# When layer 1's first edge columns are multiplied inside layer 0's last block: two sixteenths later, and nine of them behind the last expert

## The chip, the cores and the metric

The kernel runs on one NeuronCore of a Trainium2 chip. The metric is device time in microseconds (us) of one execution. The kernel before took 2913.34 us, the median of three runs from 2908.56 to 2917.24. The profile is one further execution, which took 2906.32 us, with a span of 2904.5 us from its first to its last instruction.

The engines have short names in the views: PE is TensorE (PEld its weight loads), DVE is VectorE, ACT is ScalarE, POOL is GpSimd, SP is SyncE, whose queue here only starts DMAs.

## What is computed

Two layers of a graph network with a mixture of experts behind each, on 6,250 nodes of 256 features and 100,000 edges (`src`, `dst`, `edge_weight`, sorted by `dst`). Cut to what matters:

```python
x = x + gnn0(norm(x))                       # gather h at dst, weigh, sum at src
x = x + sum_e gate[e] * mlp_e(norm(x))      # layer 0: 8 experts, all of them for every node
h1 = norm(x)
x = x + segment_sum(edge_weight * h1[src], dst) @ W + bias     # layer 1's aggregation
x = x + expert_top1(norm(x))                # layer 1: 32 small experts, the best one for each node
```

The output is x. Layer 1's aggregation needs rows of `h1` from all over the graph, while layer 0 produces them in order of nodes. This is the seam in which the change lies.

## The kernel before

**Tiles.** The nodes lie in 49 tiles of 128 in the SBUF tensor `X`, which is updated in place. Layer 0 works through them in 15 blocks of 1 to 4 tiles (`blocks0`); the last block, `late`, has three. Layer 1 has 13 blocks of its own (`blocks1`), the first of them three tiles as well.

**Edge columns.** The edges of layer 1, sorted by destination, are cut into 782 columns of 128 edges. One column is five pieces of work, issued by `columns1`:

1. `gather` (L199, its DMA at L201): GpSimd starts an indirect DMA that fetches 128 rows of `h1` from HBM into a tile `g`.
2. `weighted`, first half (L230): ScalarE multiplies `g` by the edge weight into `m[:, 0]`, rounded to fp32r.
3. `weighted`, second half (L231): VectorE computes the rest that the rounding lost into `m[:, 1]`.
4. `one_hots` (L218, L222): VectorE writes, for three columns at a time, the 0/1 matrix `s` that says which edge goes to which node.
5. The product `acc<-m,s` (L277) on TensorE, summed in PSUM over groups of eight columns.

A group that is done is moved by L250 (ScalarE) and added by L251, L255 and L258 (VectorE) into the destination tile's sums. `columns1` hands out these later steps 2, 6 and 9 columns behind the group's end. The pool for the early columns has 12 tiles `g` and 6 tiles `m` (`(3, 12, 6, 2)`: one-hots, gathers, weighted, sums), so gather number k needs the weighting of column k-12 to be over, and weighting k the product of column k-6.

**The early columns.** The first 64 columns (`NE = EARLY * GC`) belong to the first tiles of layer 1. They are multiplied already in layer 0's last block, in `first_sums`, with only those source rows that earlier blocks have written to `h1` (`early_columns` sets the weight of the others to nought). What they miss, edges that come from the last block's own nodes, is added behind that block: `missing` builds matrices for it in three steps beside experts 5 to 7 (iota L822 on GpSimd, `to_m` and `of_m` L858 to L862 on VectorE, `pm` L866 and L867 on TensorE, L868 and L869 on ScalarE), and `add_missing` multiplies them with the last block's rows (`corr` L878) and adds them to `first_sums` (L880). Tiles 0, 1 and 2 of `first_sums` go through `by_weight` (L209 to L215) before layer 1's first block can begin; parts 3 and 4 are wanted only later. A tile takes its columns from half a group before it to half a group behind it: tiles 0 to 2 are complete with the first 52 of the 64 columns.

**The order of the work.** An aggregation is a generator that hands out one column for each `next`; `Stream.upto(n)` (L367) advances it until n columns are out. `aggregate0` (L692) first hands out layer 0's own 882 columns, then the 64 early ones. The loop over experts calls `sums.upto(...)` twice for each of the 8 experts of a block, before the second hidden layer (`hidden0`, L748 and L751) and before the outputs (`outs0`, L760 and L762). These 16 places, the sixteenths of the block, take their targets from `plans[b]`. For the last block they are

```python
head = 2
plans[-1] = [cum[-1] + NE * max(0, u + 1 - head) / (2 * NX0 - 1 - head) for u in range(2 * NX0 - 1)]
plans[-1] += [cum[-1] + NE + 1]
```

so nothing in sixteenths 0 and 1, then 4.9 columns in each, and by the last sixteenth all 64 with their later steps.

The program's text is not yet the order on the engines: a scheduler in the framework takes the instructions with their priorities and their dependences and writes one fixed order for each engine, which then runs in that order, with waits on semaphores. So the plan says from where on columns may be expected, and the scheduler interleaves them.

**At the block's two ends.** The gathers of the early columns need all earlier rows of `h1`. The last of these come from `end0` of the block before (stats, the square root L333 on ScalarE, the normalized rows `hs` L771 on VectorE, the DMA L773 on SP), which runs beside the last block's first expert. At the far end `end0(late)` does the same for the last block; then follow `add_missing`, `by_weight` and `begin1`, layer 1's first block. Layer 1's own gathers read all of `h1`, so the first of them waits for that last L773. SP also carries four loads of layer 1's expert weights into the space of layer 0's: `load1`, L799 (first matrix) and L803 (second), half of each at expert 4 and half at expert 7, each as soon as the old weights have been used for the last time.

Of the kernel before, what the change touches and what calls it, by code (L numbers as in the profile page):

```python
# [24 lines left out]
CS = 8  # L25
# [8 lines left out]
NX0 = 8  # L34
# [15 lines left out]
def gnn_ffn_kernel(ctx: ExitStack, tc: tile.TileContext, a, out):  # L50
# [323 lines left out]
    def aheads(cum, parts, rests):  # L374


        cum = cum + [cum[-1]] * 2
        out, at = [], cum[0]
        for b, rest in enumerate(rests):
            head = parts - rest  # L380
            plan = [at + (cum[b + 1] - at) * (u + 1) / head for u in range(head)]
            plan += [cum[b + 1] + (cum[b + 2] - cum[b + 1]) * (u + 1) / parts for u in range(rest)]
            at = plan[-1]
            out.append(plan)
        return out
# [247 lines left out]
    NE = EARLY * GC  # L633

    with tc.tile_pool(name="layer0", bufs=1) as wp, tc.tile_pool(name="outs0", bufs=1, side="right") as wo_pool, \
# [56 lines left out]
        def aggregate0():  # L692
            for b, tiles in enumerate(blocks0):
                idx, dl, w = edges[b]
                for i, t in enumerate(tiles):
                    acc = psum.tile([P, 2, D], F32, tag="agg", name="acc", bufs=2)
                    for j in range(EW):
                        if j % SJ == 0:
                            s = one_hots(wp, dl[:, i, :], j, 3)
                        m = weighted(wp, h0, idx[:, i, j:j + 1], w[:, i, j:j + 1], 12, 6)  # L700
                        nc.tensor.matmul(acc, s[:, j % SJ, :], m, start=(j == 0), stop=(j == EW - 1))  # L701
                        if j == EW - 1:
                            for half in range(2):
                                nc.vector.tensor_add(X[:, t, :], X[:, t, :], acc[:, half, :])
                        yield

            for _ in columns1(wp, psum, range(NE), h1[:LIM, :], idx_e, w_e, (3, 12, 6, 2)):
                yield
            while True:
                yield  # L710
# [161 lines left out]
        def add_missing(hs, fs):  # L872

            corr = psum.tile([P, 2, D], F32, tag="mm", name="corr", bufs=3)
            for u, f in enumerate(fs):
                rows = min(P, NEAR - f * P)
                for i in range(n_late):
                    nc.tensor.matmul(corr[:rows, u, :], mats[i][:, f * P:f * P + rows], hs[:, i, :],  # L878
                                     start=(i == 0), stop=(i == n_late - 1))
                nc.vector.tensor_add(first_sums[:rows, f, :], first_sums[:rows, f, :], corr[:rows, u, :])  # L880


        sums = Stream(aggregate0())
        cum = [EW * (tiles[-1] + 1) for tiles in blocks0]
        plans = aheads(cum, 2 * NX0, [4] * nblk)
        head = 2
        plans[-1] = [cum[-1] + NE * max(0, u + 1 - head) / (2 * NX0 - 1 - head) for u in range(2 * NX0 - 1)]
        plans[-1] += [cum[-1] + NE + 1]
        sums.upto(cum[0])
        block = begin0(blocks0[0])  # L890
        first = hidden0(0, block, 0, block[1])
# [40 lines left out]
            next(firsts[-1])  # L932
        for part in firsts:
            next(part)
        add_missing(hs, (3, 4))
    sorted_ctx.close()


    with tc.tile_pool(name="layer1", bufs=1, reuse_waits="tile") as wp, \
# [74 lines left out]
        with tc.tile_pool(name="flow1", bufs=1, reuse_waits="tile") as flow:  # L1014

            sums = Stream(columns1(flow, psum, range(NE, NREAL), h1, src_c, val_c, (5, EW + 6, 12, 4)))
            cum = [0] + [min(CS * (2 * tiles[-1] + 2) + CS // 2, NREAL) + LAG - NE for tiles in blocks1[1:]]
            plans = aheads(cum, 2 * NC1, [4] + [8] * (len(blocks1) - 1))
# [90 lines left out]
```

## Time and profile before

| what | us |
|---|---|
| median of three runs | 2913.34 |
| profiled execution | 2906.32 |
| its span | 2904.5 |
| TensorE busy | 2685.0 (92%) |
| VectorE busy | 2017.1 (69%) |
| GpSimd busy | 1921.2 (66%) |
| ScalarE busy | 1626.5 (56%) |
| mean of one L201 gather, layer 0 and early / layer 1 | 1.02 / 1.01 |
| median from a gather's issue to its landing | 2.8 |

How to read the views: a row of a timeline gives the start in us, the busy time in us, engine, line, operation, tiles written and read, the number of instructions in a row, and in brackets the idle time before and what ended it. A row of waits gives who waited for whom, the total in us, how often, and the longest. A row of windows gives, for a stretch from one time to another, each engine's busy time with its instruction count, the granted clock of TensorE as a share of full speed, the share of the DMA engines and GB/s. In the 40 slices a digit is tenths of the slice, in the PEclk row tenths of full clock. An fp32 product shows as two records ("x8" is four products), one in fp32r as one.

The last block of layer 0 runs from about 1722 to 1835 us of the span; layer 1's first gather is issued at 1840.95 us.

### The profile page before, as it was taken

What the parts mean: (1) busy time and instruction counts of PE and PEld (TensorE: products, weight loads), DVE (VectorE), ACT (ScalarE), POOL (GpSimd) and SP (SyncE); (2) the same over time, 40 slices, a digit from 0 to 9 for tenths busy, and PEclk for the clock granted to TensorE, in tenths of its full rate; (3) what the DMA queues carried; (4) which work ended last, traced back from release to release, by engine and by line L of the source; (5) the groups of instructions that cost most, each with busy time, mean ns of one, the idle gap of its engine ahead of it and who ended that gap; (6) DMA issues with size and microseconds to landing.
All of it is one profiled execution on the core that took longest, in us unless ns stands there. A gap on an engine that the chain in (4) does not pass through costs nothing.

```text
span 2904.5 us, 36970 instructions
## 1 busy us (share of the span) xinstructions
PE 2685.0 (92%) x10276; PEld 1750.0 (60%) x10336; DVE 2017.1 (69%) x4917; ACT 1626.5 (56%) x3790; POOL 1921.2 (66%) x1932
## 2 busy tenths in 40 slices
PE   5888848889999999999999998779999999999998
PEld 2444427666566666666666665556666666666666
DVE  8999978788767767667666646566666666666630
ACT  6777837655555555555555545355555555555532
POOL 4666667777767666776675527577777777777720
PEclk9999969999999999999999998989999999999999
DMA  4000043333333333333332214333333333333310
GB/s 150 19 19 19 19 144 97 104 101 101 93 99 96 89 102 93 91 103 95 90 100 82 82 40 126 95 108 100 108 109 109 106 108 102 108 107 109 109 46 12
DMA packets 123140, 260.73 MB, mean 90 GB/s; under 512 B 32236, under 2 KB 68904, under 8 KB 122920
## 3 DMA queue, kind: packets, MB, share of 16 engines
q0 software_dynamic: 79872, 218.21, 26.5%
q1 hardware_dynamic: 31672, 32.42, 3.4%
q10 hardware_dynamic: 11376, 7.60, 0.8%
q8 instruction: 85, 1.39, 0.2%
q14 instruction: 135, 1.11, 0.1%
HBM read 238.87 MB, written 19.25 MB: 89 GB/s over the span
## 4 chain that ended last, share of the span: by engine, by line
PE 60%; DMA 10%; issue 6%; DVE 5%; ACT 3%; POOL 2%; another core or an unknown queue 0%; ACTq 0%; POOLq 0%; SPq 0%; DVEq 0%
PE ph L748 19%; PE py L760 10%; PE py L999 8%; PE ph L983 8%; PE acc L701 6%; DMA g<-h,src_c 5%; PE acc L277 4%; DMA g<-h,idx 3%; POOL g L201 2%; DVE m L231 2%; ACT m L230 2%; DMA g<-h,idx_e 1%; PE ph L214 1%; PE tr L340 1%; PE pl L720 1%
## 5 line engine op out<-in xcount | busy, mean ns | idle before, releaser
L201 POOL DMA_INDIRECT g<-h,idx x882 | 900.0, 1020 | 390.7 <-DVE m L231 171.5
L201 POOL DMA_INDIRECT g<-h,src_c x718 | 724.9, 1010 | 244.2 <-issue 110.8
L230 ACT ACTIVATE m<-g,w 128x256 fp32r<-128x256 f32 x882 | 393.9, 500 | 254.5 <-PE acc L701 130.7
L230 ACT ACTIVATE m<-g,val_c 128x256 fp32r<-128x256 f32 x718 | 349.8, 503 | 278.5 <-PE acc L277 133.2
L751 ACT ACTIVATE hT<-ph,shift,scale 128x512 f32<-128x512 f32 (+3 forms) x480 | 328.8, 696 | 313.4 <-PE ph L748 312.0
L231 DVE SCALAR_TENSOR_TENSOR m<-g,val_c,m 128x256 fp32r<-128x256 f32 x718 | 336.8, 482 | 213.0 <-ACT m L230 209.2
L231 DVE SCALAR_TENSOR_TENSOR m<-g,w,m 128x256 fp32r<-128x256 f32 x882 | 397.3, 476 | 44.4 <-ACT m L230 43.5
L748 PE MATMUL ph<-nT,w 128*128 128x512 f32 (+3 forms) x960 | 376.1, 527 | 25.0 <-ACT hT L751 24.9
L760 PE MATMUL py<-wo,hT 128*128 128x256 f32 x1568 | 379.7, 385 | 14.0 <-DVE X L762 11.4
L999 PE MATMUL py<-w,hm 128*128 128x256 f32 x1568 | 385.2, 384 | 2.0 <-ACT hm L988 1.9
L983 PE MATMUL ph<-nT,w 128*128 128x512 f32 (+2 forms) x832 | 377.2, 574 | 0.0
L701 PE MATMUL acc<-m,s 128*128 128x512 f32 x882 | 339.7, 488 | 37.1 <-DVE scale L657 24.7
L748 PE MATMUL ph<-hT,w 128*128 128x512 f32 (+3 forms) x960 | 369.9, 519 | 0.5 <-ACT hT L751 0.5
L760 PEld LDWEIGHTS py<-wo,hT 128*128 128x128 f32 x1568 | 293.2, 192 | 80.6 <-DVE X L762 28.0
L277 PE MATMUL acc<-m,s 128*128 128x512 f32 x782 | 335.4, 502 | 5.7 <-DVE m L231 5.4
L999 PEld LDWEIGHTS py<-w,hm 128*128 128x128 f32 x1568 | 290.9, 192 | 51.8 <-ACT hm L988 3.9
L222 DVE TENSOR_TENSOR s<-col,dl 128x384 fp32r<-128x384 f32 x294 | 161.3, 550 | 185.7 <-PE acc L701 183.5
L748 PEld LDWEIGHTS ph<-nT,w 128*128 128x128 f32 x960 | 176.9, 197 | 175.1 <-issue 119.6
L748 PEld LDWEIGHTS ph<-hT,w 128*128 128x128 f32 x960 | 175.7, 193 | 118.5 <-issue 89.1
L988 ACT ACTIVATE hm<-ph,b 128x512 f32<-128x512 f32 (+2 forms) x208 | 136.8, 659 | 194.7 <-PE ph L986 141.9
L701 PEld LDWEIGHTS acc<-m,s 128*128 128x128 f32 x882 | 169.2, 195 | 108.9 <-issue 50.1
L983 PEld LDWEIGHTS ph<-nT,w 128*128 128x128 f32 x832 | 158.0, 192 | 102.2 <-issue 81.8
(248 smaller groups left out, 3343.7 us busy)
## 6 DMA issues: line engine op xcount, KB each, us to landing
g<-h,idx POOLq DMA_INDIRECT x882, 2.8
g<-h,src_c POOLq DMA_INDIRECT x718, 2.8
h<-hs SPq DMA_DIRECT2D x25, 256.0 KB, 2.1
X<-in_x_dram SPq DMA_DIRECT2D x12, 512.0 KB, 9.4
out_dram<-o SPq DMA_DIRECT2D x11, 512.0 KB, 3.4
h<-hs SPq DMA_DIRECT2D x9, 512.0 KB, 3.1
w<-in_L_ffn_W_dram ACTq DMA_DIRECT2D x2, 2048.0 KB, 11.9
wo<-in_L_ffn_Wo_dram ACTq DMA_DIRECT2D x1, 2048.0 KB, 21.1
```

The source lines that it names most:

```text
L201: nc.gpsimd.indirect_dma_start(out=g, out_offset=None, in_=h, in_offset=bass.IndirectOffsetOnAxis(ap=idx, axis=0))
L222: nc.vector.tensor_tensor(s[:, :n], col[:, None, :].to_broadcast([P, n, P]), dl[:, j:j + n, None].to_broadcast([P, n, P]), OP.is_equal)
L230: nc.scalar.activation(m[:, 0, :], g, AF.Copy, scale=w)
L231: nc.vector.scalar_tensor_tensor(m[:, 1, :], g, w, m[:, 0, :], op0=OP.mult, op1=OP.subtract)
L277: nc.tensor.matmul(acc, s[:, (j - js.start) % SJ, :], m, start=opens, stop=done)
L701: nc.tensor.matmul(acc, s[:, j % SJ, :], m, start=(j == 0), stop=(j == EW - 1))
L748: nc.tensor.matmul(ph[:, :nw], (w1, w2)[layer][:, e, k, m * P:(m + 1) * P], src[:, k, :nw], start=(k == 0), stop=(k == 1))
L751: nc.scalar.activation(hT[:, m, :nw], ph[:, :nw], AF.Relu, bias=shift[:, layer, c:c + 1], scale=scale[:, layer, c:c + 1])
L760: nc.tensor.matmul(py, hT[:, k, j * P:(j + 1) * P], wo[:, e, k, :], start=(k == 0), stop=(k == 1))
L983: nc.tensor.matmul(ph[:, :nw], w1f[:, k, c * P:(c + 1) * P], nT[:, k, :nw], start=(k == 0), stop=False)
L988: nc.scalar.activation(hm[:, :nw], ph[:, :nw], AF.Relu, bias=b1[:, c:c + 1])
L999: nc.tensor.matmul(py[:, j, :], now[:, cols], w2f[:, c, :], start=False, stop=(c == NC1 - 1), skip_group_check=True)
```

## The change

The plan of the last block gets other numbers, and a line is added behind `by_weight`:

```diff
         plans = aheads(cum, 2 * NX0, [4] * nblk)
-        head = 2
-        plans[-1] = [cum[-1] + NE * max(0, u + 1 - head) / (2 * NX0 - 1 - head) for u in range(2 * NX0 - 1)]
-        plans[-1] += [cum[-1] + NE + 1]
+
+        head, tail = 4, 2 * CS
+        plans[-1] = [cum[-1] + (NE - tail + CS // 2 + 3) * max(0, u + 1 - head) / (2 * NX0 - head) for u in range(2 * NX0)]
@@ behind the last block: end0(late), add_missing for parts 0 to 2, by_weight for tiles 0 to 2
         for part in firsts:
             next(part)
+        sums.upto(cum[-1] + NE + 1)
         add_missing(hs, (3, 4))
     sorted_ctx.close()
```

With `NE` 64, `CS` 8 and `NX0` 8, the targets are: none in sixteenths 0 to 3, then 55 / 12 = 4.6 columns in each of the other twelve, so 55 by the block's end. The other nine columns, with the later steps of the last two groups, are asked for behind `by_weight`, ahead of the corrections for parts 3 and 4. The 55 take in the 52 columns of tiles 0 to 2 and the three by which their last group's sums follow.

## The prediction

> **What bounds the kernel now.** First the page's 40 slices (72.6 us each), to see where TensorE is not full.
>
> ```profile
> PE   5888848889999999999999998779999999999998
> ...
> PEclk9999969999999999999999998989999999999999
> ```
>
> Outside the sort at the start TensorE is nine tenths busy, but for three slices from the 25th on (1743 to 1960 us), where the clock dips too. That is layer 0's last block and the first two of layer 1. Next, the waits of TensorE from the last block's first hidden product (1722.3) to the first correction product (1837.05), and the busy table of the same 114.7 us.
>
> ```profile
> PE py L760 <- DVE X L762: 6.0, 2, 5.6
> PE acc L277 <- DVE m L231: 5.4, 8, 1.0
> PE ph L748 <- ACT hT L751: 4.1, 2, 2.3
> PE pm L866 <- DVE to_m L858: 3.0, 1, 3.0
> PE corr L878 <- DVE hs L771: 2.4, 1, 2.4
> PE pm L866 <- ACT wo L869: 0.7, 1, 0.7
> ```
>
> ```profile
> core 0: us, PE busy (x) PEld busy (x) DVE busy (x) ACT busy (x) POOL busy (x), PEclk, DMA share, GB/s
> 1722.30:1837.00 114.70, 92.54 (x305) 60.12 (x304) 65.54 (x164) 54.63 (x112) 66.63 (x65) 0.91 0.38 114
> ```
>
> The block's work at full clock: a burst of 4 hidden or 6 output products takes 2.58 (starts 1722.33, 1724.91, 1727.49 in the timeline); there are 8 second-layer, 7 first-layer and 8 output bursts, 59.3. 64 column products at 0.33 (1734.48 to 1734.81) are 21.1; 12 pairs of L866 and L867 at 0.35 are 4.2. Sum 84.6, and 84.6 / 0.91 = 93.0 is the busy time shown. So 114.7 is 84.6 of work, 8 of low clock and 22 of waits. Behind whom? VectorE's waits in the same stretch lead with 25.9 us for `m` on ScalarE, and ScalarE's with 35.1 us for the gathers. So GpSimd's timeline, and then the two ends on ScalarE:
>
> ```profile
> 1730.62 0.94 POOL L201 DMA_INDIRECT g<-h,idx_e  x1 [48.90 <-DVE X L762]
> 1731.87 0.95 POOL L201 DMA_INDIRECT g<-h,idx_e  x1 [0.30 <-issue]
> ...
> 1815.39 0.95 POOL L201 DMA_INDIRECT g<-h,idx_e  x1 [0.30 <-issue]
> 1840.95 0.94 POOL L201 DMA_INDIRECT g<-h,src_c  x1 [24.62 <-PE corr L878]
> ```
>
> ```profile
> 1765.31 1.84 ACT L230 ACTIVATE m<-g,w_e 128x256 fp32r<-128x256 f32 x4 [4.24 <-DMA g<-h,idx_e]
> ...
> 1820.94 0.51 ACT L230 ACTIVATE m<-g,w_e 128x256 fp32r<-128x256 f32 x1 [3.49 <-DMA g<-h,idx_e]
> ...
> 1836.13 0.20 ACT L333 ACTIVATE rstd<-rstd 128x3 f32<-128x3 f32 x1 [3.90 <-DVE rstd L332]
> ```
>
> The 64 gathers start at 1730.62 (block 11's rows of h1 must be in HBM: hs at 1727.3 and a DMA of 2.52), run without a gap beyond 0.30, and the last is issued at 1815.39: 84.8 / 63 = 1.35 us each. A column can become a product 3.9 us after its gather starts (1730.62 to 1734.48). The plan of before asks for products from the third sixteenth on, when not one is ready, and then for 5 a sixteenth: TensorE meets the gathers head-on. The two long landings (ScalarE rows 1 and 2) sit at the loads of L799, issued at 1758.37 and 1815.02; the chain shows gathers of 6.31 and 5.47 there, against 2.74 elsewhere. The L803 load at 1773.50 left none over 3.0.
>
> **The change, part by part.** Nothing is added or removed: 64 columns keep their 64 gathers, weightings, one-hots and products, and the queues of SP and GpSimd keep their order but for the iota of L822, which stands behind gather 43 instead of 53. From the norm of layer 1's first block on, the order of all four engines' instructions in the two built programs is the same. So all of it lies between 1733 and about 1850, and what the last block ends earlier, layer 1 starts earlier.
>
> *Products from the fifth sixteenth.* Four sixteenths now run as bare bursts: 1722.33 + 6 x 2.58 = 1737.8, and the fourth column is due at 1734.5 + 3 x 1.25 = 1738.2. The 5.4 us of L277 waits become 0.5. They don't all come back, since later groups of 4 to 5 columns (9.2 per expert, 12.3 us of gathers against 3 x 2.58 + 9.2 x 0.33 = 10.8 of TensorE) again catch up with the gathers. Also ScalarE's order now puts all four relu evictions of an expert behind a run of five or six weightings (the first run ends with column 10, landed about 1745), so the second first-layer burst waits for its PSUM tile there, some 3 us, then 1 to 2 per expert. I charge these to the gather's pace, not twice.
>
> *Nine columns behind the last expert.* In the built program the scheduler pulls five of the nine up again, so 60 products precede the corrections and 4 (1.3 us) follow the first three `by_weight`. TensorE's floor to product 60 is 59.3 + 60 x 0.33 + 4.2 = 83.3, or 1805.6. Its walk with the waits: the first `pm` needs the iota, behind gather 43 at 1730.6 + 43 x 1.33 = 1788, so it runs at 1789; from there 14 outputs (6.0), 12 hidden products (7.7), `pm` (4.2) and 24 columns (7.9), with 1.5 of waits on `to_m`, give 1816.3, and 1815.3 for the last output.
>
> *What sets the end instead.* In ScalarE's order the square root L333 of the last norm now stands behind the weightings of all 64 columns and one eviction (before, weighting 64 was 15 us earlier). A rule of the Trainium skill speaks against the change here: TensorE: Matmul & The Clock Gate, section "Architectural detail", says that ScalarE's and VectorE's queues are strict FIFO. The row agrees in kind: the `m` at 1820.94 held the evictions behind it for 3.49. Without the rule, VectorE's own chain decides: 1.4 from the last output to the root, as before (1834.7 to 1836.1), and four weightings (columns 58 to 61) that now stand between, spaced 0.40: 1815.3 + 1.4 + 1.6 = 1818.3, -17.8. With it: gather 64 issued at 1815.4 as now (nothing upstream of it changes), landed 2.74 later (the second L799 load moves from 1815 to about 1798, off the last gather), weighting 0.51, eviction 0.36, a hand-over of 0.2, so L333 at 1815.4 + 2.7 + 0.5 + 0.4 + 0.2 = **1819.2** against 1836.13: **-16.9**. I take the rule's value.
>
> *Costs.* One VectorE add (L251, 0.42) now stands between reciprocal and hs. Behind hs, L255, two `m` and one `s` (0.41 + 0.96 + 0.55) fall into the 1.74 us in which VectorE waited for corr. Another L251 (0.42) stands ahead of layer 1's reciprocal. The four late products go before corrections that no one waits for. Together +0.8. SP: h1's last rows are written right after hs in both; layer 1's first gather came 3.3 after that issue (1837.66 to 1840.95) and moves along.
>
> *The clock.* The same page, Part 1, says that TensorE falls to half rate after about 3.4 us of idling and needs as long to recover. Here: after the waits around 1751 a burst of 8 records took 4.17 instead of 2.74, 1.4 lost; the rule gives up to 1.7 per lull. The 5.63 lull at 1761 is of that kind, and the change has one such (column 10). By either it is 1.4 to 1.7 on TensorE, early, where the gathers bound; so 0 on the sum, and 2 if it falls after 1789.
>
> Sum: -16.9 + 0.8 = -16.1. The profiled execution took 2906.32 (span 2904.5 and 1.8 around it); the median is 7.0 above it. Against its own time the sum gives 2890.2; off the median, **2897**. Runs spread over 8.7 us, so about 0.3% is what can be told from no change.
>
> **Rivals.**
>
> *A, gathers pace the end* (above): 2897; own range 2892 to 2902. For it: 0.30 gaps throughout, 35.1 us of ScalarE waits.
>
> *B, gathers get faster.* With VectorE and DMA less crowded they keep the early 1.25 (1730.62 to 1731.87): gather 64 at 1730.6 + 78.8 = 1809.4, L333 at 1813.2, -22: 2891. Against it: layer 1's mean is 1.01 + 0.30 too.
>
> *C, half comes back.* Evictions behind weightings, one more lull after 1789 and the L799 load hitting columns 50 to 53 make TensorE the last, by 9 us (three recoveries of 1.4 and an L799 wait of 5): L333 at 1828, 2906.
>
> *D, slower: the ring of buffers.* Gather k needs weighting k-12, and that product k-18. Where TensorE falls over 18 columns behind, gathers stop, and it then waits for them. Break-even is L333 at 1835.3, that is the last gather landing 16 later than 1818.1, or 1.6 us per gather instead of 1.35; at 1.75 the result is 2922. Against it: gather 19 needs product 1, done at 1738 and wanted at 1755; gather 64 needs product 46, done by 1807 in the walk and wanted at 1815.
>
> *E, the wait only moves.* Layer 1's gathers start from other releases and begin1 takes the gain back: 2913. Against it: the order there is the same and its first gather is released by hs's write.
>
> **How the numbers follow.** A 0.58, B 0.13, C 0.19, D 0.06, E 0.04. Faster by over 0.3% (under 2904.6): nearly all of A (0.56), B, and 0.08 of C, 0.77. Slower (over 2922): most of D, 0.05. The rest 0.18. The range 2889 to 2910 holds A, most of B (0.10) and C (0.16).
>
> **What would show it.** Right: first `acc` L277 of the last block at about 1738, L277 waits under 2 us in its first ten columns; last early gather at 1813 to 1817; L333 at 1817 to 1822 with ScalarE's `m` waiting for a gather just ahead; first layer-1 gather near 1824.5. Wrong: a gap over 0.30 between early gathers (D), TensorE waits on `hT` over 12 us or the last outputs well after the last gather's landing (C), or a layer-1 first gather at 1824 with an unchanged end (E).

## The result, and the profile after

The changed kernel takes 2898.59 us (median of eight runs, 2893.99 to 2904.92) against 2912.36 us for the kernel before in the same series (eight runs, 2906.32 to 2917.24). The ratio is 0.9955, with a 95% interval of 0.9943 to 0.9967, so about 13 us less (9.6 to 16.6). Forecast were 2897.0 us and -16.1. A later series gave 2895.83 against 2909.19, ratio 0.9953 (0.9935 to 0.9972). The profiled execution took 2895.13 us, its span is 2893.4.

First the 40 slices of the page of the changed kernel.

```profile
PE   5888848888999999999999998779999999999998
...
PEclk9999978999999999999999999999999999999999
```

The dip behind the 24th slice is still there in TensorE's busy share (8779), but the clock row no longer dips with it. In the fine view this is, from the last block's first hidden product to the first correction product (1726.50 to 1824.14), first TensorE's waits and then the row of windows:

```profile
PE py L760 <- DVE X L762: 4.4, 2, 2.5
PE ph L748 <- ACT hT L751: 3.9, 2, 2.1
PE acc L277 <- DVE m L231: 1.7, 4, 0.8
PE pm L866 <- DVE to_m L858: 1.6, 2, 1.0
```

```profile
1726.50:1824.14 97.64, 84.23 (x301) 56.91 (x301) 61.61 (x159) 52.91 (x111) 66.04 (x65) 0.97 0.43 134
```

The same stretch was 114.70 long with a busy TensorE of 92.54 at a clock of 0.91. TensorE's work in front of the corrections is smaller by only four products (1.3 us). All else in the 17 us is less waiting (13.4 us not busy instead of 22.2, so 8.8) and, as the rest, about 7 us of less low clock.

The stretch starts 4.2 us later in this profile than in the one before (first early gather at 1734.85 instead of 1730.62), after 1.7 ms of unchanged instructions. So times are counted from here on from the first early gather. Now GpSimd's timeline of the changed kernel, the end of ScalarE's, and two rows of TensorE's:

```profile
1734.85 0.94 POOL L201 DMA_INDIRECT g<-h,idx_e  x1 [48.89 <-DVE X L762]
...
1819.01 0.95 POOL L201 DMA_INDIRECT g<-h,idx_e  x1 [0.30 <-DVE X L762]
1828.05 0.95 POOL L201 DMA_INDIRECT g<-h,src_c  x1 [8.09 <-PE corr L878]
```

```profile
1819.80 0.51 ACT L230 ACTIVATE m<-g,w_e 128x256 fp32r<-128x256 f32 x1 [1.63 <-DMA g<-h,idx_e]
1821.58 1.31 ACT L230 ACTIVATE m<-g,w_e 128x256 fp32r<-128x256 f32 x3 [1.28 <-DMA g<-h,idx_e]
1822.79 0.36 ACT L250 ACTIVATE first_sums<-acc 128x256 f32<-128x256 f32 x1
1823.06 0.19 ACT L333 ACTIVATE rstd<-rstd 128x3 f32<-128x3 f32 x1
```

```profile
1818.87 1.13 PE L760 MATMUL py<-wo,hT 128*128 128x256 f32 x4
...
1824.14 1.13 PE L878 MATMUL corr<-hs,wo 128*128 128x256 f32 x4 [1.70 <-DVE hs L771]
```

The gathers run as they did (84.16 us from first to last, before 84.77, every gap 0.30). But the root L333 now follows the last weighting by 0.17 us. The last output of expert 7 (ended 1819.99) no longer decides.

In the kernel before, the last gather's column sat in the middle of the last expert's work. This is VectorE's timeline there, and then two rows of TensorE's:

```profile
1821.49 0.48 DVE L231 SCALAR_TENSOR_TENSOR m<-g,w_e,m 128x256 fp32r<-128x256 f32 x1 [3.12 <-ACT m L230]
1821.89 0.87 DVE L762 SCALAR_TENSOR_TENSOR X<-py,gate,X 128x256 f32<-128x256 f32 x2
1822.67 0.51 DVE L858 TENSOR_SCALAR to_m<-wo,dst_m 128x576 fp32r<-128x576 f32 x1
```

```profile
1823.24 0.50 PE L866 MATMUL pm<-to_m,of_m 128*128 128x512 f32 x1 [3.01 <-DVE to_m L858]
...
1831.35 3.33 PE L760 MATMUL py<-wo,hT 128*128 128x256 f32 x12
```

Read it as a chain: the last gather lands, ScalarE weighs it (the `m` at 1820.94 of the prediction's view), VectorE's `m` follows at 1821.49, behind it in VectorE's queue the `X` adds and then `to_m`, and on that waits TensorE's `pm` at 1823.24. Only then come the rest of the missing rows' products, four columns, expert 7's second layer, its outputs and the statistics. From the end of the last weighting to L333 it is 14.7 us.

The marks of all profiles, in us from the start of the first early gather. "Weighting 64" is the end of ScalarE's last `m`, "last output" the end of expert 7's last product, "sel" the first product of layer 1 with `sel` (L987 in the changed kernel, L986 in the kernel before):

| kernel | last gather issued | weighting 64 | last output | L333 | sel |
|---|---|---|---|---|---|
| before | 84.77 | 90.83 | 104.06 | 105.51 | 129.29 |
| changed | 84.16 | 88.04 | 85.15 | 88.21 | 112.37 |
| changed, again (e5) | 84.17 | 88.08 | 85.15 | 88.25 | 112.36 |
| head alone (e11) | 87.32 | 92.58 | 105.82 | 107.27 | 131.37 |
| *chips with late gathers:* | | | | | |
| head alone (e1 / e6) | 97.3 / 98.1 | 104.9 / 105.6 | 117.2 / 117.8 | 118.6 / 119.3 | 144.2 / 144.8 |
| tail alone (e2 / e7 / e12) | 97.2 / 99.5 / 98.3 | 113.8 / 112.3 / 110.9 | 113.0 / 111.5 / 110.1 | 115.4 / 114.0 / 112.6 | 141.9 / 140.0 / 138.7 |
| tail held behind (e3 / e8) | 97.4 / 101.6 | 116.4 / 120.2 | 105.3 / 109.1 | 106.8 / 110.5 | 134.0 / 137.1 |
| half the gathers (e4 / e9 / e10) | 60.5 / 60.1 / 59.0 | 85.4 / 84.9 / 83.8 | 83.9 / 83.5 / 82.4 | 86.7 / 86.3 / 85.1 | 113.4 / 110.6 / 111.1 |

Ten of the twelve experiments ran on four other chips, on which the kernel before takes 3228 to 3296 us and gathers are issued with gaps of up to 7 us (the last section has more on them). They are compared only among themselves.

### The profile page after: what moved, and what is told of

Same layout as the page of the kernel before. It is cut to its first block, busy times and chain, and to the rows that moved or that the text cites. A ratio compares the mean times of both kernels' runs of the same rounds, so it can differ in the third digit from the quotient of the medians.

```text
span 2893.4 us, 37030 instructions
## 1 busy us (share of the span) xinstructions
PE 2677.7 (93%) x10336; PEld 1750.2 (60%) x10336; DVE 2012.4 (70%) x4917; ACT 1626.1 (56%) x3790; POOL 1926.1 (67%) x1932
## 4 chain that ended last, share of the span: by engine, by line
PE 65%; DVE 17%; DMA 8%; issue 4%; ACT 4%; POOL 1%; ACTq 0%; POOLq 0%; DVEq 0%
PE ph L748 19%; PE py L760 10%; PE py L1000 9%; PE ph L984 9%; PE acc L701 6%; PE acc L277 4%; DMA g<-h,src_c 4%; DMA g<-h,idx 3%; DVE loads L527 3%; DVE to L523 2%; DVE m L231 2%; ACT m L230 2%; PE ph L987 1%; PE ph L214 1%; POOL g L201 1%
## 5 line engine op out<-in xcount | busy, mean ns | idle before, releaser
L748 PE MATMUL ph<-nT,w 128*128 128x512 f32 (+3 forms) x960 | 373.1, 524 | 25.0 <-ACT hT L751 24.8
L760 PE MATMUL py<-wo,hT 128*128 128x256 f32 x1568 | 382.1, 387 | 13.8 <-DVE X L762 10.5
L984 PE MATMUL ph<-nT,w 128*128 128x512 f32 (+2 forms) x832 | 374.8, 571 | 0.0
L748 PE MATMUL ph<-hT,w 128*128 128x512 f32 (+3 forms) x960 | 368.5, 518 | 0.5 <-ACT hT L751 0.5
L277 PE MATMUL acc<-m,s 128*128 128x512 f32 x782 | 332.2, 499 | 1.7 <-DVE m L231 1.7
L748 PEld LDWEIGHTS ph<-nT,w 128*128 128x128 f32 x960 | 175.2, 195 | 174.2 <-issue 118.1
L748 PEld LDWEIGHTS ph<-hT,w 128*128 128x128 f32 x960 | 176.2, 193 | 118.9 <-issue 88.3
L984 PEld LDWEIGHTS ph<-nT,w 128*128 128x128 f32 x832 | 157.2, 191 | 101.5 <-issue 81.1
## 6 DMA issues: line engine op xcount, KB each, us to landing
w<-in_L_ffn_W_dram ACTq DMA_DIRECT2D x2, 2048.0 KB, 11.2
```

Of the source, the lines that this page charges most:

```text
L277: nc.tensor.matmul(acc, s[:, (j - js.start) % SJ, :], m, start=opens, stop=done)
L748: nc.tensor.matmul(ph[:, :nw], (w1, w2)[layer][:, e, k, m * P:(m + 1) * P], src[:, k, :nw], start=(k == 0), stop=(k == 1))
L760: nc.tensor.matmul(py, hT[:, k, j * P:(j + 1) * P], wo[:, e, k, :], start=(k == 0), stop=(k == 1))
L984: nc.tensor.matmul(ph[:, :nw], w1f[:, k, c * P:(c + 1) * P], nT[:, k, :nw], start=(k == 0), stop=False)
```

## The experiments

**The changed kernel again (e5)**, with no edit.

> The changed kernel itself once more. If the chip is one with the times of the case (kernel before near 2912 us), L333 is again 88 us after the first early gather, within 1 us, and the ratio is 0.995 to 0.997. If it is the chip of the experiments so far (kernel before 3284 us, its gathers issued with gaps of up to 6 us where the other had 0.30), theory A says that the end follows the gathers' slower pace in both kernels: L333 100 to 107 us after the first early gather, where head alone had 118.6 and tail alone 115.4, and a gain over the kernel before of 8 to 15 us, 0.995 to 0.998; a rival in which TensorE's own work and waits set the end says 115 or more and no measurable gain.

Measured: 2895.83 against 2909.19, 0.9953 (0.9935 to 0.9972). The marks repeat within 0.05 us. So on such a chip a difference of half a microsecond in them means something, though the whole time spreads over 6 to 17 us from run to run.

**The head alone (e11, e1, e6)**: products from the fifth sixteenth, all 64 columns ahead of expert 7's output as before.

```diff
-        head, tail = 4, 2 * CS
-        plans[-1] = [cum[-1] + (NE - tail + CS // 2 + 3) * max(0, u + 1 - head) / (2 * NX0 - head) for u in range(2 * NX0)]
+        head = 4
+        plans[-1] = [cum[-1] + NE * max(0, u + 1 - head) / (2 * NX0 - 1 - head) for u in range(2 * NX0 - 1)]
+        plans[-1] += [cum[-1] + NE + 1]
...
-        sums.upto(cum[-1] + NE + 1)
```

> The products come from the fifth sixteenth, but all 64 columns stay ahead of the last expert's output and nothing is left behind by_weight. Measured from the start of the first early gather to the end norm's root (L333): 105.5 us in the kernel before, 88.2 in the changed one. Theory A (the 64 gathers pace the end: a head that comes later costs and gains TensorE nothing that the gathers don't give back): the last column's product can be fed about 87 us after the first gather, and the last 12 products of expert 7 and the statistics (some 6 us) follow it: L333 at 93 to 95, so about -11 us, time near 2901. Rival (the head saves only its 5.4 us of waits for m, the rest is the tail's): L333 at 100, time near 2907. Rival C (the head's waits only move elsewhere): L333 at 104 or more, time 2911 to 2914.

> The head part alone, again, where the kernel before takes some 2910 us (on the chip of the first four runs gathers waited for buffers, and both theories' numbers were off). From the first early gather to L333: before 105.5 us, changed kernel 88.2, twice within 0.05. Theory A (gathers pace the end, then expert 7's last outputs): 93 to 95, time 2899 to 2901. Rival (the head saves its 5.4 us of waits for m): 100, time near 2906. Rival C (the waits only move): 104 or more, time 2908 to 2912.

> The head part alone, for a chip on which gathers are issued 0.30 us apart. From the first early gather to L333: kernel before 105.5 us, changed kernel 88.2. Theory A (gathers pace the end, then expert 7's last outputs): 93 to 95, time near 2900. Rival (the head saves its waits for m, 5.4 us, and the tail the rest): 100, time near 2906. Rival C (the waits only move): 104 or more, time 2908 to 2912. If the gathers are late here as on three chips of four so far, L333 is at 118 to 120 again and the time is within 0.3% of the kernel before.

Measured on a chip of the case's kind (e11): 2914.03 against 2909.47, ratio 1.0013 (1.0000 to 1.0026), L333 at 107.27, which is 1.76 later than before. None of the gain is there. Of the three numbers offered for L333, that of rival C holds ("the waits only move"; its time of 2908 to 2912 is passed by 2 us), but for another reason than C's. Its TensorE waits, its row of windows and the end of its ScalarE timeline:

```profile
PE ph L748 <- ACT hT L751: 6.7, 3, 3.0
PE acc L277 <- DVE m L231: 6.0, 2, 4.0
PE py L760 <- DVE X L762: 5.4, 3, 2.6
PE pm L866 <- DVE to_m L858: 3.2, 2, 2.5
PE corr L878 <- DVE hs L771: 2.4, 1, 2.4
```

```profile
1725.68:1842.17 116.49, 92.72 (x306) 61.95 (x304) 65.88 (x164) 54.37 (x112) 69.28 (x65) 0.90 0.38 112
```

```profile
1824.51 0.51 ACT L230 ACTIVATE m<-g,w_e 128x256 fp32r<-128x256 f32 x1 [3.78 <-DMA g<-h,idx_e]
1825.65 0.91 ACT L230 ACTIVATE m<-g,w_e 128x256 fp32r<-128x256 f32 x2 [0.62 <-DMA g<-h,idx_e]
...
1841.25 0.20 ACT L333 ACTIVATE rstd<-rstd 128x3 f32<-128x3 f32 x1 [3.90 <-DVE rstd L332]
```

The waits for `m` did not fall from 5.4 to 0.5; they are 6.0. With the same 64 columns in two sixteenths less, the plan asks for 5.8 of them a sixteenth instead of 4.9 and runs into the gathers a little later and harder. And from the end of weighting 64 (92.58) to L333 (107.27) it is 14.69 us, in the kernel before 14.68 (90.83 to 105.51). As long as all 64 columns stay ahead of expert 7's output, the end hangs on the last gather by the same chain, with either head. The 1.76 us by which it is later are the 1.75 by which weighting 64 is. They come from gathers issued later (2.55 at the last one): two of them took 4.06 and 2.92 us of GpSimd's time, where the longest in the changed kernel is 1.73. The 93 to 95 that I had for theory A had put 6 us of work behind the last column instead of 14.7.

On the chips with late gathers (e1, e6) the ratios are 0.9992 (0.9964 to 1.0019) and 0.9993 (0.9961 to 1.0026), no difference either. L333 lies 13.7 and 13.6 us behind weighting 64.

**The tail alone (e2, e7, e12)**: the last nine columns behind the last expert, products from the third sixteenth as before.

```diff
-        head, tail = 4, 2 * CS
+        head, tail = 2, 2 * CS
```

> The products start two sixteenths earlier, as in the kernel before, and the last nine columns lie behind the last expert. Theory A (the gathers pace the end): TensorE pays its waits for m in the first bursts but catches up while the last gathers land; L333 at 88 to 90 us after the first early gather (changed kernel 88.2), time within 2 us of the changed kernel, near 2899. Rival C (TensorE's own work and waits set the end): the 5.4 us of waits for m and 1 to 3 us for hT come back, L333 at 93 to 96, time near 2905.

> The tail part alone, again. Theory A (the gathers pace the end): L333 at 88 to 90 us after the first early gather, time within 2 us of the changed kernel, near 2897. Rival C (TensorE's own work and waits set the end): 5.4 us of waits for m and some for hT come back, L333 at 93 to 96, time near 2902.

> The tail part alone, for a chip on which gathers are issued 0.30 us apart; the head alone had L333 at 107.3 us after the first early gather there (kernel before 105.5, changed kernel 88.2), ratio 1.0013: nothing of the gain. Theory A (the tail carries it; the gathers pace the end whatever the head): L333 at 88 to 90 us, time within 2 us of the changed kernel, near 2897. Rival C (the head is worth something only with the tail: products that come two sixteenths earlier make TensorE wait for m, 5.4 us, and the waits are not made up before expert 7's outputs): L333 at 93 to 96, time near 2902. If the gathers are late here, L333 is at 114 to 115 again.

All three ran on chips with late gathers: 0.9986 (0.9964 to 1.0009), 0.9971 (0.9951 to 0.9990) and 1.0012 (0.9988 to 1.0036). That is one gain of 0.1 to 0.5% and two that can't be told from nothing. In the marks one thing is as in the changed kernel: the last output comes 0.8 us ahead of the end of weighting 64 instead of 12.2 behind it (e1, e6), and L333 is 3.1 and 5.3 us earlier than with the head alone on the same chips (e2 against e1, e7 against e6). But the gathers do not set the end there. Weighting 64 ends 12.6 to 16.6 us after the issue of the last gather (7.5 and 7.6 with the head alone), and in all three runs the last weightings wait for products to free a tile `m` (for e2 the row at 2014.01 further down). So at the end it is TensorE that the weightings wait for, which is nearer to rival C than to theory A. How much of TensorE's delay goes back to earlier late gathers is not shown. GpSimd's timeline of e2 shows why the numbers expected for the other chip don't apply:

```profile
1965.09 0.95 POOL L201 DMA_INDIRECT g<-h,idx_e  x1 [0.30 <-issue]
1970.68 0.94 POOL L201 DMA_INDIRECT g<-h,idx_e  x1 [4.64 <-DVE m L231]
```

The ring of twelve gather buffers is full, and GpSimd waits for a weighting to free one. From first to last the gathers take 97.2 to 99.5 us, 1.54 to 1.58 each: near the 1.6 that the prediction named as the break-even of its rival D. What the tail alone does where gathers are not late is left open, and with it whether the later head adds anything once the tail has moved.

**The tail held behind the norm (e3, e8)**: the changed kernel, in which the nine tail columns stand behind L333 in ScalarE's order and behind the last hs in VectorE's.

```diff
-        hs = end0(late)
+        hs, behind = end0(late), list(held)
...
-        sums.upto(cum[-1] + NE + 1)
+        with tc.issue_after(behind[0].ins), tc.issue_after(behind[1].ins):
+            sums.upto(cum[-1] + NE + 1)
```

(`held` keeps the instructions of L333 and L771.)

> The changed kernel, with the nine tail columns' weightings held behind the end norm's root on ScalarE and behind its hs on VectorE, so that L333 waits for no gather after column 54. Theory A (in-order queues: L333 stands behind the weightings of all 64 columns): L333 comes 2 to 6 us earlier, at 82 to 86 us after the first early gather, the corrections and layer 1's first gather with it, time 2894 to 2897. Rival C (TensorE's last outputs set L333, the weightings ahead of it are hidden): L333 at 87 to 88 and the nine columns then come later than before, so that by_weight and begin1 wait: time 2898 to 2904.

> The nine tail columns' weightings held behind the end norm's root on ScalarE and behind its hs on VectorE, again. Theory A (L333 stands behind 64 weightings): L333 at 85 to 86.5 us after the first early gather instead of 88.2 (expert 7's last output ended at 85.15 in the changed kernel with two products ahead of it), the corrections 2 us earlier; and the first layer-1 gather 2 us earlier, at 91. What the nine columns then cost behind the corrections was 3 us on the other chip (24.2 us from L333 to layer 1's first sel product became 27.3): time between the changed kernel's and 2 us more. Rival C (TensorE's last outputs set L333): L333 at 87.5 or later, time 2 to 4 us above the changed kernel.

The numbers of both theories miss, since gathers were late. What can be read is the order of queues. ScalarE's timeline at the end of e2 (tail alone) with the row of L332, on which L333 waits, and ScalarE's of e3:

```profile
2014.01 0.51 ACT L230 ACTIVATE m<-g,w_e 128x256 fp32r<-128x256 f32 x1 [0.62 <-PE acc L277]
2015.51 0.38 ACT L250 ACTIVATE first_sums<-acc 128x256 f32<-128x256 f32 x1 [0.99 <-PE acc L277]
2016.20 0.20 ACT L333 ACTIVATE rstd<-rstd 128x3 f32<-128x3 f32 x1 [0.32 <-DVE rstd L332]
```

```profile
2015.63 0.46 DVE L231 SCALAR_TENSOR_TENSOR m<-g,w_e,m 128x256 fp32r<-128x256 f32 x1
2016.00 0.17 DVE L332 TENSOR_SCALAR rstd<-mv 128x3 f32<-128x3 f32 x1
```

```profile
1994.40 0.20 ACT L333 ACTIVATE rstd<-rstd 128x3 f32<-128x3 f32 x1 [4.22 <-DVE rstd L332]
1994.51 2.49 ACT L230 ACTIVATE m<-g,w_e 128x256 fp32r<-128x256 f32 x6
```

With the weightings out of its way, L333 comes 1.45 and 1.44 us behind the last output, as in the kernel before (1.45). With the weightings ahead of it, it comes 2.46, 2.47 and 2.46 behind (e2, e7, e12), and 3.06 in the changed kernel. So standing behind the weightings costs L333 1.0 us there and 1.6 here. The 1.0 us there are VectorE's: L333 waits for L332, which stands behind the `m` of the last columns in VectorE's queue, and not for ScalarE's own queue. From L333 to the first sel product the held order then takes 27.3 and 26.6 us instead of 26.0 to 26.4, so it gives back 0.2 to 1.3. The times, 0.9980 (0.9956 to 1.0005) and 0.9978 (0.9957 to 1.0000), don't differ measurably from the tail alone. That its last output is earlier too (105.3 and 109.1) has two possible causes, the later head and the two products less ahead of it, and these runs don't part them.

**Half the gathers (e4, e9, e10)**: one early gather for two columns; weightings, one-hots and products all stay.

```diff
-                m = weighted(pool, h, idx[:, j:j + 1], w[:, j:j + 1], ahead, parts)
+                m = weighted(pool, h, idx[:, j:j + 1], w[:, j:j + 1], ahead, parts,
+                             kept_g[0] if first and j % 2 else None, kept_g)
```

> Leaves out every second early gather: each gather's rows serve two columns, so the sums are not the reference's; weightings, products and everything else stay. Theory A (64 gathers of 1.32 us pace the end): with 32 of them L333 falls to what TensorE alone needs, 78 us after the first early gather (10 us less than the changed kernel). Rival C (TensorE and its waits on hT, X and the missing rows set the end): L333 falls by less than 3 us, to 85 to 88.

> Leaves out every second early gather (a gather's rows serve two columns, so the sums are not the reference's), again. Theory A (64 gathers pace the end): L333 falls to what TensorE alone needs, 75 to 80 us after the first early gather. Rival C (TensorE and its waits on hT, X and the missing rows set the end): L333 falls by less than 3 us, to 85 to 88.

> Leaves out every second early gather (a gather's rows serve two columns, so the sums are not the reference's), for a chip on which gathers are issued 0.30 us apart, as in the case's two profiles (L333 88.2 us after the first early gather, twice within 0.05). Theory A (64 gathers pace the end): L333 falls to what TensorE alone needs, 75 to 80 us. Rival C (TensorE and its waits on hT, X and the missing rows set the end): L333 falls by less than 3 us, to 85 to 88. On the two chips with late gathers it was 86.7 and 86.3, 28 us below the tail alone, which says A there; if it is 86 here too, TensorE's chain and the gathers are level in the changed kernel.

L333 is at 86.7, 86.3 and 85.1 us, against 112.6 to 115.4 with the tail alone and 118.6 to 119.3 with the head alone on such chips (this kernel has the head and the tail). Its nearest relative with both, the tail held behind, has 106.8 and 110.5 on the chips of e4 and e9, so L333 fell by 20 and 24 us. The whole time fell too: 3238.68 against 3284.11, 3263.68 against 3296.45, 3263.64 against 3291.64, one run each of this kernel, with the kernel before alone spreading over 31 and 48 us in the first two series and measured once in the third. Where gathers are late, they pace this seam. But L333 does not fall to 75 to 80, as theory A had it; it lies in the 85 to 88 of rival C. All waits over the stretch, in e10:

```profile
POOL g L201 <- DVE m L231: 20.0, 12, 6.2
...
PE ph L752 <- ACT hT L755: 6.7, 1, 6.7
```

(Lines stand four further down in this kernel: L752 is L748.) GpSimd is no longer what the others run after: it is held by its ring of buffers. TensorE's last output still ends at 82.4 to 83.9, with 10.8 to 11.2 us of waits ahead of it, 0.9 for `m` and the rest for `hT`, `X` and `to_m` (in e4 4.5 us have no releaser in the trace). The changed kernel has 11.6 there. The floor of 1805.6 us in the prediction, 75 after the first early gather, counted work without such waits. A gather that landed late may be behind the 6.7 us for `hT`, since that relu stands behind weightings in ScalarE's queue; the trace does not show it.

Set beside the changed kernel, where the last output ends at 85.15: by itself it would allow L333 at 85.15 + 1.45 = 86.6, and at 85.15 + 2.46 = 87.6 with the weightings in VectorE's queue. So gathers (88.2) and TensorE (86.6 to 87.6) are almost level there. That is an estimate from two kinds of chip. It says that another gain at this place needs both.

## Why the prediction was right

*Gathers pace the end (rival A, the forecast).* Right. L333 was forecast at 1819.2; with the 4.2 us by which this profile runs later, 1823.4; measured 1823.06. By length: -16.9 forecast, -17.3 measured (105.51 to 88.21). The split can now be given: 14.5 us are the work that stood behind the last weighting (14.68 before, 0.17 after), and 2.8 the earlier end of that weighting, 0.6 from the issue of the last gather (84.77 to 84.16) and 2.2 from what follows it (from that issue to the end of its weighting 6.06, now 3.88). The head alone, with its unchanged 14.69, is what shows that the 14.5 go with the tail. That the sum comes so near is in part luck, for three small misses nearly cancel: the last gather was issued 0.6 us earlier, the end of its weighting came 3.88 us after that instead of 3.2, and L333 0.17 us after this end instead of 0.6.

*Products from the fifth sixteenth.* "The 5.4 us of L277 waits become 0.5" fails as a statement on this part: 1.7 with the tail, 6.0 without. The prediction left this gain out of its sum ("I charge these to the gather's pace"), so nothing follows for the time. The first L277 was forecast at 1738, or 1742.2 with the shift, and came at 1745.62:

```profile
1744.11 2.07 PE L760 MATMUL py<-wo,hT 128*128 128x256 f32 x4 [2.53 <-DVE X L762]
1745.62 2.01 PE L277 MATMUL acc<-m,s 128*128 128x512 f32 x4
```

TensorE waited 2.53 us for `X`, since that add stood behind the `m` of an early column in VectorE's queue. I had walked ScalarE's queue there and not VectorE's. The 3 us foreseen for `hT` at column 10 came later and smaller (1.80 at 1763.24 and 2.06 at 1787.04).

*Nine columns behind the last expert.* Right, and it is the part without which nothing is gained. Whether it gains all of it without the head was not measured on a chip of the case's kind. The walk gave the last output 1815.3; with the shift 1819.5, measured 1819.99.

*The end set by ScalarE's queue.* The rule of the Trainium skill (TensorE: Matmul & The Clock Gate, section "Architectural detail") and the row agree in kind: L333 starts right behind the eviction that follows the 64th weighting. The size is small, by VectorE's rows:

```profile
1821.90 0.45 DVE L231 SCALAR_TENSOR_TENSOR m<-g,w_e,m 128x256 fp32r<-128x256 f32 x1
1822.27 0.16 DVE L332 TENSOR_SCALAR rstd<-mv 128x3 f32<-128x3 f32 x1
```

VectorE's chain of `m` rows put L332 at 1822.27. In the kernel before L333 came 0.2 us behind L332, so without ScalarE's queue it would have come about 0.6 us earlier than 1823.06. The difference of the two forecasts was 0.9.

*The loads.* "The second L799 load moves to about 1798, off the last gather": issued 1803.69, so 1799.5 without the shift. Missed was the load behind it, which had come at 1831.55 and is now issued while the last gathers land:

```profile
1803.69 0.71 SPq L799 DMA_DIRECT2D w<-in_L_ffn_W_dram  x1
1815.63 0.38 SPq L803 DMA_DIRECT2D w<-in_L_ffn_W_dram  x1
```

The weightings of columns 61 and 62 waited 1.63 and 1.28 us for theirs; the gather issued at 1816.51 landed 4.99 us later. The prediction had cleared this kind of load with "The L803 load at 1773.50 left none over 3.0". That reading was wrong: in the same profile the gather issued at 1773.18 landed 6.01 us later. That the load is the cause was not tested. Without these waits, the last gather (1819.01) would have landed 2.74 later at 1821.75 and been weighed at 1822.26, not at 1822.89: 0.6 us, an estimate.

*Costs, +0.8.* From L333 to the first sel product it is 24.16 us instead of 23.78, and to the first L983 product (L984 in the changed kernel) 20.05 instead of 19.18 (1855.31 - 1836.13): 0.4 to 0.9.

*The clock, 0 on the sum.* The granted clock of the stretch rose from 0.91 to 0.97 (0.97 again in e5). Of TensorE's 8.3 us less busy time, 1.3 are the four products and about 7 the clock. That is much more than one lull of 1.4 to 1.7. The head alone kept the low clock (0.90) with its waits. What the 7 us are worth was not measured: in the changed kernel the gathers set the end, but had TensorE ended 0.6 to 1.6 us later, they would count. So the zero is right for the end, and its margin thin: with the low clock kept, TensorE would have set the end, some 5 to 6 us later (7 less the 0.6 to 1.6), an estimate. That is rival C by another road than its three lulls.

*The other rivals.* B, gathers at 1.25 us: no, 1.34. C: `hT` waits 3.9 us, far from 12. D, the ring: no gap over 0.31 between early gathers on this chip; on the others, gaps of 4 to 7 us. E: layer 1's first gather moved from 110.33 to 93.20, and the end moved with it.

*From -16.1 to about -13.* The profiled seam gives -17.3 + 0.4 = -16.9 to the first sel product, and from there to the end it is 1046.2 us instead of 1044.6 (e5 has 1044.8, e11 1044.9, so most of that 1.6 is that one execution). The medians say -13.8 and, in the later series, -13.4. The three profiles of changed programs (changed, again, head alone) reach the first early gather at 1734.0 to 1736.5, the single one of the kernel before at 1730.62. If that is the program, it explains the missing 3 us; if it is chance, the interval of the first series ends at -16.6, just short of the -16.9. One profile of the kernel before doesn't tell, and it stays open.

## What to carry to other kernels

When a stream of transfers paces a seam, look at what stands in the in-order queues behind its last element: that work is what can be gained, 14.5 of 17.3 us here, and a later start of the stream's consumers with that work left in place was worth nothing (1.0013). What the later start is worth once the work has moved is not known from these runs. Walk every queue that the element passes (here VectorE's `m`, `X`, `to_m`, and from there TensorE's `pm`), since an add for one purpose becomes late by waiting behind a multiply for another. And ask of a moved load not only where it goes but what the load queued behind it will now meet.

## What the runs showed of the hardware

The same program can meet a different machine: on the chips of e5 and e11, as in the case's own profiles, the kernel before takes about 2910 us, on four others 3228 to 3296, with rows of ScalarE and VectorE that take as long as before (a weighting about 500 ns), a mean granted clock of 0.93 to 0.94 instead of 0.97, and gathers that stall GpSimd's ring: its wait for `m` is 483.1 us in e1 against 228.3 in e11, the same program. What makes them late is not shown. The traces from these chips hold no landing times, and waits of ScalarE's `m` of up to 18.4 us have a releaser that is not in them (95.4 us in all in e1). That gathers are part of it is seen from half the gathers, which took 28 to 45 us off the whole time. Head alone, tail alone and tail held behind came to 0.997 to 1.001 of the kernel before there; the changed kernel itself wasn't run there.

On one kind of chip the seam repeats almost to the hundredth: two profiles of the changed kernel, from different series, have L333 at 88.21 and 88.25 us and the sel product at 112.37 and 112.36. Differences that the whole time can't resolve can be read there.

Among the early gathers, one that normally takes 0.95 us of GpSimd's time took 4.06 and 2.92 in the head alone, 2.69 in the kernel before, and at most 1.73 in the changed one. The 4.06 one, issued at 1762.38, lies beside a stretch in which VectorE ran almost without a pause (1761.11 to 1765.62). The cause was not tested.
